# A fused attention and FFN block on one core: one root for the last normalisation, rows less means beside the power, and the last products by tile

## The chip, the cores and the metric

The kernel runs on one core of one Trainium2 chip. The metric is device time in microseconds (us) of one execution, of which several are taken; the profile is one more execution, recorded by the hardware profiler. The engines are named as in the profile: PE (TensorE, with PEld for its weight loads), DVE (VectorE), ACT (ScalarE), POOL (GpSimd) and SP (SyncE, which here only issues transfers).

## The reference

The input x holds 16 sequences of 256 rows and 256 columns, in float32. Two residual blocks follow each other, each normalised before and after:

```
x = x + layernorm(attention(layernorm(x)))
x = x + layernorm(ffn(layernorm(x)))

layernorm(x) = (x - mean(x)) / sqrt(var(x) + 1e-5)          # over the 256 columns

attention:  q = x @ Wq.T                  16 heads of 128, rotary embedding
            kp, vp = x @ Wkv.T            one key and value shared by the heads
            kh, vh = per-head factors: a cumulative sum over rows with learned decay
            k = kp * kh (rotary), v = vp * vh
            p = softmax(causal(q k / sqrt(128)));   o = p v;   o @ Wout.T

ffn:        gate, up = split(x @ ternary(w_gate_up).T)       1024 each
            h  = silu(gate) * up
            hn = h / sqrt(mean(h * h) + eps)                 # rms_norm, eps of float32
            hn @ ternary(w_proj).T
```

`ternary` quantises weights in groups of 64 to -1, 0 or 1 times the group's mean magnitude. The last layernorm works on rows that the rms_norm has scaled by one factor each, 1 / sqrt(mean(h*h) + eps).

## The kernel before

The 16 sequences go in 8 pairs. A pair and a head make a slot (128 slots, about 8.07 us each), and in each slot PE computes the scores of one head, the outputs of the head before it, the queries of the next one, and pieces of projections and of the FFN. DVE takes the exponent's maximum and the rotary products, ACT the exponents, the division by the softmax's total (L722) and the copies of outputs (L801, `oT`), POOL the products that make keys and values (L658 `kT`, L770 `vph`). SP issues nearly all transfers, among them those that transpose the probabilities.

The order on each engine is the order in which the program is written. Inside a slot there are places (`first`, `scored`, `turned`, `emptied`, `projection`, `last`), and `put(slot, place, steps, key=...)` hangs a step into one of them. The table `MOVED` shifts a step by its key, in sixths of a slot. Keys beginning with P and Q belong to the next pair's preparation (`keep` is ACT's copy of the normalised rows L391, `nor` the normalisation with POOL's power L260 and product L300), keys with T to the twelve blocks of ternary weights that are quantised during pair 0 (`narrow` L207, a POOL cast; `magnitudes` L197 on ACT; `compare` L215 to L221 on DVE; `combine` L227 to L230 on POOL; `write` L233, an ACT cast), keys with Y12 to the FFN of sequence 12.

[...]

The last normalisation never scales its rows by the rms factor: with acc the projection of the unscaled h, `inv` = (ss/1024 + eps)^-0.5 is computed on POOL (`inverse_roots`), and the rows' own factor from var(acc) * inv^2 (`last_factors`, or `end_factors` and `end_scales` for the last three). `inverse_root` (L254) is one POOL power, with an addition of eps ahead of it where one is asked for. `Rows` holds mean and variance of tiles of 128 rows: `bn_stats` (L271), `bn_aggr` (L273), `shifts` (L285: minus mean times factor, on DVE) and `apply_on_act` (L290).

The FFNs of the last three sequences, 13 (`c`), 14 (`a`) and 15 (`b`), run behind the last head in the function `end`, in an order written out by hand, with the steps of sequence 12 and of older work between them (`rest`). Each of them ends with `end_rows` (L1060): ACT scales and shifts the two tiles from PSUM, DVE adds the residual `xt` (L1076), SP stores each tile (L1077). Sequences 0 to 12 end with `finish` (L1033) and `store`.

## Time and profile before

| | |
|---|---|
| time, three executions | 1088.61, 1088.84, 1090.61 us (median 1088.84) |
| profiled execution | 1088.68 us, span of its instructions 1086.9 us |
| mean granted clock of PE | 0.996 |
| busy: PE, PEld, DVE, ACT, POOL | 1067.8, 854.5, 846.2, 736.2, 689.9 us |
| costliest PE lines (share of the chain that ended last) | L324 queries 19%, L830 output projection 18%, L670 scores 14% |
| first PE instruction, end of the last matmul, end of the span | 1.35, 1079.34, 1086.9 us |

The span runs from the first to the last recorded instruction; the execution's own time has 1.8 us more around it. The profile's chain of waits follows the work that ended last back from its end. An idle time in brackets behind a row of the timeline is the engine's idle time ahead of that row, with what released it. Ends of matmuls are modelled, so that two matmuls in a row overlap by a little.

### The profile page before, as it was taken

What the parts mean: (1) busy time and instruction counts of PE and PEld (TensorE: products, weight loads), DVE (VectorE), ACT (ScalarE), POOL (GpSimd) and SP (SyncE); (2) the same over time, 40 slices, a digit from 0 to 9 for tenths busy, and PEclk for the clock granted to TensorE, in tenths of its full rate; (3) what the DMA queues carried; (4) which work ended last, traced back from release to release, by engine and by line L of the source; (5) the groups of instructions that cost most, each with busy time, mean ns of one, the idle gap of its engine ahead of it and who ended that gap; (6) DMA issues with size and microseconds to landing.
All of it is one profiled execution on the core that took longest, in us unless ns stands there. A gap on an engine that the chain in (4) does not pass through costs nothing.

```text
span 1086.9 us, 18506 instructions
## 1 busy us (share of the span) xinstructions
PE 1067.8 (98%) x5704; PEld 854.5 (79%) x5704; DVE 846.2 (78%) x2308; ACT 736.2 (68%) x2153; POOL 689.9 (63%) x761
## 2 busy tenths in 40 slices
PE   9999999999999999999999999999999999999997
PEld 6777767788788877888778887788878888788897
DVE  6888989877887769878788777977788777877474
ACT  4877766666776658576585765866677665767664
POOL 5966897338655676458665576665865556747354
PEclk9999999999999999999999999999999999999998
DMA  6312134455444444444353444445434444443201
GB/s 230 110 53 77 61 112 155 133 159 142 141 141 133 145 136 146 139 129 151 122 154 123 151 137 131 150 132 156 131 133 144 132 133 137 145 142 97 69 1 39
DMA packets 108626, 137.35 MB, mean 126 GB/s; under 512 B 12208, under 2 KB 76208, under 8 KB 108528
## 3 DMA queue, kind: packets, MB, share of 16 engines
q1 hardware_dynamic: 105696, 129.02, 38.6%
q0 software_dynamic: 2000, 6.56, 1.8%
q8 instruction: 46, 0.75, 0.3%
q10 hardware_dynamic: 832, 0.59, 0.2%
q14 instruction: 52, 0.43, 0.1%
HBM read 88.41 MB, written 47.71 MB: 125 GB/s over the span
## 4 chain that ended last, share of the span: by engine, by line
PE 88%; DVE 6%; ACT 2%; DMA 1%; POOL 1%; issue 1%; SPq 0%; ACTq 0%; POOLq 0%; DVEq 0%
PE qps L324 19%; PE att L830 18%; PE sps L670 14%; PE ops L786 9%; PE ffn L977 6%; PE ups L884 5%; PE gps L884 5%; PE ops L793 5%; PE hg L324 1%; PE vps L324 1%; DVE turned_q L346 1%; PE kp L324 1%; DVE prob L683 1%; PE tps L756 1%; DMA moved<-sq 1%; DVE qps L354 1%
## 5 line engine op out<-in xcount | busy, mean ns | idle before, releaser
L683 DVE CUSTOM_DVE_ANT_0 prob<-sps,mask 128x128 f32<-128x128 f32 (+1 forms) x512 | 160.9, 354 | 123.2 <-PE sps L670 120.1
L801 ACT COPY oT<-ops 128x512 f32<-128x512 f32 x128 | 75.0, 586 | 258.0 <-PE ops L793 258.0
L324 PE MATMUL qps<-xnT,wq_sb 128*128 128x512 f32 x512 | 241.8, 594 | 0.8
L693 ACT ACTIVATE prob<-prob,low 128x128 f32<-128x128 f32 (+1 forms) x512 | 225.7, 444 | 18.6 <-DVE low L683 18.3
L830 PE MATMUL att<-wout_sb,oT 128*128 128x256 f32 x1024 | 237.7, 379 | 0.0
L830 PEld LDWEIGHTS att<-wout_sb,oT 128*128 128x128 f32 x1024 | 188.4, 190 | 30.2 <-issue 8.6
L770 POOL TENSOR_TENSOR vph<-vp,vh 128x512 f32<-128x512 f32 x110 | 116.2, 1056 | 128.9 <-PE ops L793 124.3
L670 PE MATMUL sps<-kT,qT 128*128 128x128 f32 (+1 forms) x1024 | 192.0, 330 | 4.3 <-DVE qT L357 2.1
L346 DVE TENSOR_TENSOR turned_q<-qps,sin_sb 64x512 f32<-64x512 f32 (+1 forms) x258 | 176.0, 682 | 15.8 <-PE qps L324 10.6
L658 POOL TENSOR_TENSOR kT<-kh,kr 128x512 f32<-128x512 f32 x128 | 165.0, 1290 | 4.2 <-PE sps L670 3.5
L722 ACT ACTIVATE even<-prob,total 128x128 f32<-128x128 f32 (+1 forms) x440 | 163.9, 447 | 1.1 <-DVE total L704 1.1
L670 PEld LDWEIGHTS sps<-kT,qT 128*128 128x128 f32 x1024 | 145.0, 191 | 21.2 <-issue 8.0
L324 PEld LDWEIGHTS qps<-xnT,wq_sb 128*128 128x128 f32 x512 | 95.2, 190 | 71.7 <-issue 61.6
L786 PE MATMUL ops<-pT,vph 128*128 128x256 f32 x440 | 131.4, 380 | 1.3 <-issue 0.7
L930 POOL TENSOR_TENSOR lo<-h,hi 128x512 fp32r<-128x512 f32 x54 | 69.0, 1277 | 89.1 <-ACT hi L928 89.1
L729 DVE STREAM_TRANSPOSE sq<-even 128x768 f32<-128x768 f32 x110 | 107.4, 977 | 13.5 <-ACT even L722 10.9
L693 ACT ACTIVATION_READ_ACCUMULATOR prob<-prob,low 128x1 f32 x512 | 97.0, 189 | 0.0
L354 DVE TENSOR_TENSOR qps<-qps,cos_sb 128x512 f32<-128x512 f32 (+1 forms) x129 | 89.4, 693 | 4.6
L793 PEld LDWEIGHTS ops<-pT,vph 128*128 128x128 f32 x440 | 83.5, 190 | 11.4
L357 DVE TENSOR_TENSOR qT<-qps,turned_q 128x512 f32<-128x512 f32 (+1 forms) x129 | 88.4, 685 | 4.5
L948 POOL TENSOR_TENSOR squares<-squares,sq 128x512 f32<-128x512 f32 x39 | 49.7, 1276 | 63.3 <-ACT sq L947 63.3
L793 PE MATMUL ops<-pT,vph 128*128 128x128 f32 x440 | 84.5, 274 | 0.0
(170 smaller groups left out, 1946.6 us busy)
## 6 DMA issues: line engine op xcount, KB each, us to landing
moved<-sq SPq DMA_DIRECT2D x110, 384.0 KB, 2.3
pT<-moved SPq DMA_DIRECT2D x440, 96.0 KB, 2.2
kh<-rows SPq DMA_DIRECT2D x126, 256.0 KB, 3.4
xt<-in_x_dram SPq DMA_DIRECT2D x15, 256.0 KB, 3.0
out_dram<-y POOLq DMA_DIRECT2D x13, 256.0 KB, 3.3
wout_sb<-in_wout_dram SPq DMA_DIRECT2D x2, 1024.0 KB, 9.7
w_gu<-in_wgu_dram POOLq DMA_DIRECT2D x8, 256.0 KB, 3.5
wq_sb<-in_wq_dram SPq DMA_DIRECT2D x1, 1536.0 KB, 10.4
```

Source lines behind the costliest of these rows:

```text
L324: nc.tensor.matmul(ps, lhs[:, c, :], rhs[:, c, :], start=(c == 0), stop=(c == EC - 1))
L346: self.engine.tensor_mul(by_sequence(self.turned[a : a + HALF, :]), by_sequence(self.src[b : b + HALF, :]), over_sequences(sin_sb[b : b + ...
L658: nc.gpsimd.tensor_mul(self.kT, self.kh, self.pair.kr)
L670: nc.tensor.matmul(sps[:, cols], self.qT[:, n0 + i * P : n0 + (i + 1) * P], self.kT[:, n0 : n0 + (i + 1) * P], start=True, stop=True,)
L683: nc.vector.tensor_tensor_reduce(out=prob[:, cols], in0=sps[:, cols], in1=mask[:, P - i * P :], scale=-SCALE, scalar=F32_MAX, op0=ALU.add, ...
L693: nc.scalar.activation(prob[:, cols], prob[:, cols], AF.Exp, bias=low[:, i : i + 1], scale=-1.0, accum_out=self.total[:, b * 2 + i : b * 2 ...
L722: nc.scalar.activation(dst, src, AF.Copy, scale=self.total[:, 2 * b + i : 2 * b + i + 1])
L770: nc.gpsimd.tensor_mul(self.vp, self.pair.vp, self.pair.vh[:, :, self.h : self.h + 1].to_broadcast([P, NT, D]),)
L786: nc.tensor.matmul(ops[:, n0 : n0 + N], self.vp[:, b * (N // P), :], early, start=True, stop=False,)
L793: nc.tensor.matmul(ops[:, n0 + P : n0 + N], self.vp[:, b * (N // P) + 1, :], late, start=False, stop=True,)
L830: nc.tensor.matmul(self.acc[:, t, :], oT[:, n0 + t * P : n0 + (t + 1) * P], wout_sb[:, h, :], start=(h == 0 and t == 0), stop=(h == H - 1) ...
L884: nc.tensor.matmul(ps[:, k, :], wgu_sb[:, c, (f0 + k) * P : (f0 + k + 1) * P], part[:, c, :], start=(i == 0), stop=(i == len(steps) - 1),)
```

## The change

Four things are changed. The first is arithmetic: (acc - mean) * inv / sqrt(var * inv^2 + e) is (acc - mean) / sqrt(var + e / inv^2), and 1 / inv^2 is ss/1024 + eps. So `sums_done` computes `floor` = e * (ss/1024 + eps) in one DVE operation, as before, and `last_factors` and `end_factors` take one power of var + floor. The power of ss, its square and two products by it are gone for every sequence.

The second is in the last three sequences: `end_rows` is cut in `end_centred`, which makes the rows less their mean (ACT for 13 and 14, DVE from PSUM for 15) and can run while POOL takes the power, and `end_rows`, where one DVE operation multiplies by the factor and adds the residual. All of these and the moments can be called for one tile of 128 rows.

The third is the order in `end`: c.ups(3) stands between the two transposes, b.pieces(3) ahead of the sums, a.pieces(1) later, and the last chunks of a and b are projected tile by tile (`project_rows`), with the moments and factors of each tile called between them.

The fourth is in the table `MOVED`.

```diff
 # in MOVED, entries changed or new
-    "P.keep1": 4, "Q.nor1": -1, "T7.wr": 4, "Y12.pj1": -1, "Y12.sq3": 3,
+    "P.keep1": 2, "Q.nor1": 5, "T7.wr": 7, "Y12.pj1": 2, "Y12.sq3": 1,
+    "T1.ma": -6, "T2.ma": -1, "T2.wr": 4,
...
+        def project_tile(self, u, k, t):
+            for i, part in enumerate(self.hi_lo[u]):
+                nc.tensor.matmul(self.acc[:, t, :], part[:, k, t * P : (t + 1) * P],
+                                 wproj_sb[:, 2 * u + k, :], ...)
+        def project_rows(self, t):
+            for k in range(2):
+                self.project_tile(FC // 2 - 1, k, t)
...
         def sums_done(self):
-            self.inv = small.tile([P, 2], F32, tag="inv", name=f"inv_{self.q}")
+            self.floor = small.tile([P, 2], F32, tag="inv", name=f"floor_{self.q}")
             nc.vector.tensor_scalar(
-                self.inv, self.ss, 1.0 / FF, RMS_EPS, ALU.mult, ALU.add
+                self.floor, self.ss, LN_EPS / FF, LN_EPS * RMS_EPS, ALU.mult, ALU.add
             )
-        def inverse_roots(self):
-            ...
         def last_factors(self):
             rows = self.last
             rows.minus_mean()
-            nc.gpsimd.tensor_mul(rows.rs, rows.mv[:, :, 1], self.inv2)
-            inverse_root(rows.rs, rows.rs, LN_EPS)
-            nc.gpsimd.tensor_mul(rows.rs, rows.rs, self.inv)
+            nc.gpsimd.tensor_add(rows.rs, rows.mv[:, :, 1], self.floor)
+            inverse_root(rows.rs, rows.rs, 0.0)
             nc.gpsimd.tensor_mul(rows.nm, rows.nm, rows.rs)
...
+        def end_moments(self, *some):
+            ...
+            for t in some:
+                nc.vector.bn_stats(part, self.acc[:, t, :])
+                nc.vector.bn_aggr(self.mv[:, t, :], part)
+        def end_factors(self, *some):
+            at = slice(some[0], some[-1] + 1)
+            nc.vector.tensor_add(self.rs[:, at], self.mv[:, at, 1], self.floor[:, at])
+            inverse_root(self.rs[:, at], self.rs[:, at], 0.0)
+            if self.q < B - 1:
+                nc.vector.tensor_scalar_mul(self.nm[:, at], self.mv[:, at, 0], -1.0)
+        def end_centred(self, *some):
+            for t in some:
+                if self.q < B - 1:
+                    nc.scalar.activation(self.y[t], self.acc[:, t, :], AF.Identity,
+                                         bias=self.nm[:, t : t + 1])
+                else:
+                    nc.vector.tensor_scalar_sub(self.y[t], self.acc[:, t, :],
+                                                self.mv[:, t, 0:1])
+        def end_rows(self, *some):
+            for t in some:
+                nc.vector.scalar_tensor_tensor(self.y[t], self.y[t], self.rs[:, t : t + 1],
+                                               xts[self.q][:, t, :], ALU.mult, ALU.add)
+                nc.sync.dma_start(out=out[self.q, t * P : (t + 1) * P, :], in_=self.y[t])
...
 def end():
         a.transpose()
+        c.ups(3)
         b.transpose()
...
         b.split()
-        c.ups(3)
         c.square(1)
...
         a.project(0)
-        a.pieces(1)
         b.project(0)
         b.pieces(1)
-        c.end_scales()
+        c.end_centred(0, 1)
         a.gates(2)
         a.gates_done(2)
+        a.pieces(1)
...
         b.add_squares(3)
+        b.pieces(3)
         a.sums_done()
-        a.inverse_roots()
         b.sums_done()
-        b.inverse_roots()
-        a.project(3)
-        b.pieces(3)
-        b.project(2)
-        a.last_moments()
-        b.project(3)
-        a.end_factors()
-        b.last_moments()
-        a.end_scales()
-        b.end_factors()
-        a.end_rows()
-        b.end_scales()
-        b.end_rows()
+        a.project_rows(0)
+        a.project_rows(1)
+        a.end_moments(0)
+        a.end_moments(1)
+        a.end_factors(0)
+        a.end_factors(1)
+        a.end_centred(0)
+        a.end_centred(1)
+        b.project(2)
+        b.project_rows(0)
+        b.end_moments(0)
+        a.end_rows(0)
+        b.end_factors(0)
+        b.project_rows(1)
+        a.end_rows(1)
+        b.end_moments(1)
+        b.end_factors(1)
+        b.end_centred(0)
+        b.end_centred(1)
+        b.end_rows(0)
+        b.end_rows(1)
```

## The prediction

> **What bounds the kernel now.** I read the page first, then the waits of PE, the chain of waits, and the timeline wherever the first two name a place. Line numbers are of the kernel before; a number with L is a line, the others are us from the span's start.

> ```profile
> PE 1067.8 (98%) x5704; PEld 854.5 (79%) x5704; DVE 846.2 (78%) x2308; ACT 736.2 (68%) x2153; POOL 689.9 (63%) x761
> PEclk9999999999999999999999999999999999999998
> ```

> PE is busy 98% of 1086.9 us and the diff takes no matmul away, so all that can be won is PE's idle time, its slow clock, and what lies behind its last matmul. PE ends at 1079.34: the tail is 7.57 us, and the idle time ahead of it sums to 11.5 us. The waits of PE say where:

> ```profile
> PE sps L670 <- DVE qT L357: 2.1, 2, 1.5
> PE sps L670 <- DVE total L704: 2.1, 3, 0.9
> PE tp_f L317 <- ACT xn_f L290: 1.4, 2, 1.3
> PE ops L786 <- ACT pT L761: 1.0, 2, 0.8
> PE tps L756 <- ACT prob L722: 0.2, 1, 0.2
> ```

> The columns are us in total, times, longest. The third row is the largest that the change touches; PE's timeline puts it at 1043, in the hand-ordered end, behind which PE has under 0.2 us of idle:

> ```profile
> 1043.21 0.33 PE L317 MATMUL tp_f<-ident,xn_f 128*128 128x128 f32 x1 [1.28 <-ACT xn_f L290]
> 1043.70 0.55 PE L317 MATMUL tp_f<-ident,xn_f 128*128 128x128 f32 x3 [0.16 <-ACT xn_f L290]
> ```

> The chain of waits gives the tail, from the last 24 projections on:

> ```profile
> 1074.86 4.49 PE ffn L977 x24
> ...
> 1079.37 0.76 DVE st_c L271 x2
> ...
> 1080.63 1.03 ACT y L1068 x2
> ...
> 1082.41 0.56 ACT y L1068
> ...
> 1083.46 0.42 DVE y L1076
> ```

> Between PE's end and the last add everything is serial on DVE and ACT, the two sequences one after the other; 3.02 us from the add's end (1083.88) to the span's end are the store.

> **Part 1: PE's gap at 1043.** The change puts c.ups(3) (8 matmuls, 0.12 us apart in L884's rows) between the two transposes. Its inputs are long there, and the 1.28 us gap holds its 0.96 us: **0.96**, since PE is filled from here to its end and the matmuls are missed nowhere later (the waits of later pieces have 0.2 to 2 us to spare in the trace). c's own last rows and a.pieces(1) change places among DVE's and ACT's work 15 to 30 us ahead of the end; SP issues the same six stores in the same order. Their readers have that slack too: nothing.

> The rest of the gap is a chain that begins ten us earlier:

> ```profile
> 1033.61 1.28 POOL L948 TENSOR_TENSOR squares<-squares,sq 128x512 f32<-128x512 f32 x1
> 1033.66 1.25 DVE L285 SCALAR_TENSOR_TENSOR nm_b<-mv_b,rs_b 128x2 f32<-128x2 f32 x1 [1.15 <-POOL rs_b L260]
> ```

> A two-column operation that takes 0.16 us at 1082.21 takes 1.25 here, and ends with POOL's add. ACT and DVE then run back to back from 1034.95 to xn_f. Y12.sq3 puts ACT's square ahead of oT_14, so this add runs before the power and POOL's fold (0.74 in its rows) stands here instead: nm_b ends 0.54 sooner, and with it xn_f: **0.54**. [...] PE's idle from 1041 to 1044 is 0.13, 1.28 and 0.16, so 1.50 of 1.57 are taken. Lower bound nothing (xn_f is late for another reason), upper 1.57.

> **Part 2: pair 0.** Four moves touch PE's small waits there.

> ```profile
> 43.70 2.00 DVE L221 SCALAR_TENSOR_TENSOR t_gu<-t_gu 128x512 bf16<-128x512 bf16 x1
> 43.85 1.28 POOL L658 TENSOR_TENSOR kT<-kh,kr 128x512 f32<-128x512 f32 x1
> 48.21 0.70 PE L786 MATMUL ops<-pT,vp 128*128 128x256 f32 x2 [0.80 <-ACT pT L761]
> ```

> L221 takes 0.69 where POOL is quiet. With Q.nor1 at 5, POOL makes a cast and kT_4 ahead of rs_a1, which may bring the blocked compare up to 0.8 us forward, and with it the scores, pT and the 0.80 us wait: 0 to 0.8. T7.wr takes a 0.62 us ACT cast from in front of the divides at 127.1 (PE waits 0.18 and 0.07 for them) into an ACT gap of 1.38 us: 0.25 to 0.45. T1.ma moves an ACT copy into a gap of 0.8 us, T2.wr costs 0.5 at one divide that PE's own 0.87 wait at 83.03 swallows, P.keep1 moves an ACT copy within slack, T2.ma leaves its engine's order as it is: nothing each; without that cover T2.wr costs its 0.5. Of 0 to 1.1 I take **0.7**.

> **Part 3: four small POOL operations per sequence gone** (power 0.70, two products, an addition of 0.2; some 1.3 us for each of q = 0 to 12). POOL is busy 63%, its first reader is `finish` a slot (8.07 us) later, and PE waits for no such tile: nothing. Y12.pj1 moves 8 matmuls behind tps_14 and leaves the 0.72 us wait at 1023.47 as it is.

> **Part 4: the tail.** Call X the end of the first 20 of the last 24 matmuls, 1078.68. Before, it goes: 4 matmuls 0.66, two bn_stats and aggregations to X+1.67, two factors and a shift to X+1.91, then for b the power (0.69) beside a's rows, ACT 1.02 to X+4.75, DVE's second add to X+5.20, and 3.02: X+8.22.

> After, tile 0 of b is complete at X, and the build shows that the four matmuls of tile 1 now wait for its bn_stats (a new PE wait): bn_stats 0.03 to 0.47, PE 0.52 to 1.18 instead of 0 to 0.66. Only those four matmuls are queued behind it. On DVE meanwhile: aggregation (0.18), a's first row, rs_b0, a's second row to X+1.50, bn_stats of tile 1 to 1.85, aggregation and rs_b1 to 2.25; two subtractions from PSUM (L1033 is the nearest row: 0.53 each, 0.43 apart) to 3.10; two final rows to X+3.91, and 3.02: X+6.93. The final operation, a product and sum over 256 columns from SBUF, has no row: between L1076's 0.43 (two inputs) and the 0.56 of ACT's pass; I take 0.45, being nearest to the add. The power of b1 (2.33 to 3.02) hides behind the subtractions with 0.1 to 0.4 us to spare; uncovered it costs 0.7 at most. Gain **1.29**, bounds 0.6 to 1.6; I count 1.25.

> **Sum.** 0.96 + 0.54 + 0.7 + 1.25 = 3.45, from the profiled execution's 1088.68 (span 1086.9 and 1.8 around it; the median of the runs is 0.16 above): **1085.2**.

> **The rivals.**

> *The slow clock falls elsewhere.* In the windows:

> ```profile
> 1075.50:1079.00 3.50, 3.50 (x19) 3.50 (x18) 1.54 (x7) 0.00 (x0) 2.51 (x5) 0.51 0.00 0
> ```

> The last columns are granted clock 0.51, DMA share, GB/s. From 1075.5 to 1078.9 PE runs at half clock, 16 projections 0.213 apart instead of 0.12: 1.4 us lost, after 2.6 us of one-column ss_late matmuls. With the end 2.2 us earlier and PE's gap filled, this stretch may miss the projections: 1083.8. [...] Against: ss_late's order is unchanged. 0.12.

> *PE's gap is not filled to profit*: silu or the split of a becomes late, PE stalls at the next user as long. Then 1.50 of the sum goes: 1086.7, no change. For: ACT and DVE run back to back in 1034 to 1042. Against: PE's next waits have slack. 0.16.

> *Slower: compares caught by POOL in pair 0.* Moving Q.nor1 and the casts shifts POOL against DVE in slots 2 to 16. Of the 24 compares (L218, L221), those at 42.42, 43.70, 113.15 and 127.30 are stretched by POOL from 0.69 to 1.4 to 2.1; some that now run free (57.9, 69.2, 84.0, 148.3) may be caught, 1.35 us each, and DVE's scores stand behind them and PE behind those. Without part 2's 0.7 the gain is 2.75: three caught give 1090.0, four 1091.3, slower by over 0.2%. For: pair 0 holds all long PE waits. Against: the changed order touches few of those slots. 0.10.

> *DVE locked out in the tail.* a's second row (two SBUF inputs) is issued while POOL takes b0's power; were it held for the power's 0.69, with PE's tile 1 behind, 0.8 of the tail's gain goes: 1086.0. Against: at 1081.22 DVE adds took 0.43 us beside that same power. [...] 0.06.

> **How the numbers follow.** My forecast has 0.56: with its unknowns (part 2 from 0 to 1.1, tail 0.6 to 1.6) 1084.4 to 1086.7. With the rivals at 1083.8, 1086.0 and most of 1086.7, the range is 1083.0 to 1087.8 with some 0.85 in it. 0.2% of 1088.84 is 2.2 us, about what a measurement of this kernel can tell from no change: faster means under 1086.66. Forecast 0.54, clock 0.12, lock 0.05 and a quarter of the gap case make 0.75; the rest of that case and the milder catches make "same" 0.17, the catches 0.08.

> **What would show it.** Right: tp_f of the last sequence with under 0.2 us of wait and ffn_13 after it about 1.5 us earlier for the whole end; nm_b under 1 us; the wait at 48.21 under 0.5; a tail of 7.0 us or less behind PE's tile-0 matmuls; PE's end near 1077. Wrong: new PE waits on L683's scores between 20 and 150, a PE gap moved to the first ups of a or b, or b1's power behind both subtractions.

## The result, and the profile after

The changed kernel takes 1085.41 us (median of 6, 1084.36 to 1087.19) against 1089.64 (median of 6, 1088.27 to 1090.61): a ratio of 0.9961, 95% interval 0.9949 to 0.9973. Forecast were 1085.2, within 1083.0 to 1087.8. The profiled execution takes 1085.46 with a span of 1083.7, 3.2 us shorter than before's 1086.9, and the forecast's 3.45 was made against that execution. The medians differ by 4.2 because three of those six runs of before lie at 1090.5; 63 later runs of it, taken beside the experiments, have medians of 1088.4 to 1088.6 and reach from 1086.98 to 1091.71. Where this scatter comes from is the subject of the last experiments.

Line numbers after the change are one higher up to L960 and differ behind it. The page's busy times of the changed kernel:

```profile
PE 1067.4 (98%) x5704; PEld 854.3 (79%) x5704; DVE 846.4 (78%) x2306; ACT 734.5 (68%) x2151; POOL 670.7 (62%) x705
```

Rows of the waits of PE (us in total, times, longest):

```profile
PE sps L671 <- DVE qT L358: 2.2, 2, 1.5
PE sps L671 <- DVE total L705: 1.6, 3, 0.9
...
PE tp_a L318 <- DVE xn_a L301: 1.1, 2, 0.8
PE ops L787 <- ACT pT L762: 0.8, 2, 0.6
...
PE ffn L981 <- DVE st_c L1064: 0.5, 1, 0.5
PE tp_f L318 <- ACT xn_f L291: 0.2, 1, 0.2
```

PE does the same work in the same busy time; POOL lost 56 operations and 19 us that nobody waits for. The 1.4 us wait for xn_f is 0.2, and a new wait of 0.5 for bn_stats has come. The wait for xn_a is longer than before's 0.3, but its longest piece, 0.76, lies at 6.94, among the loads of the start. The timeline at the two operations that led to the former gap (POOL's, DVE's) and at the gap itself (PE):

```profile
1033.04 0.73 POOL L997 TENSOR_TENSOR squares<-squares 128x256 f32<-128x256 f32 x1
...
1033.09 0.70 DVE L286 SCALAR_TENSOR_TENSOR nm_b<-mv_b,rs_b 128x2 f32<-128x2 f32 x1 [1.17 <-POOL rs_b L261]
...
1042.14 0.98 PE L318 MATMUL tp_f<-ident,xn_f 128*128 128x128 f32 x4 [0.19 <-ACT xn_f L291]
```

The two-column operation still ends with POOL's, which is now the short fold: 0.70 instead of 1.25 us. The tail in the chain of waits:

```profile
1072.78 3.61 PE ffn L981 x20
...
1076.42 0.44 DVE st_c L1064
...
1076.91 1.24 PE ffn L981 x4
...
1078.16 0.45 DVE st_c L1064
...
1079.01 0.45 DVE y L1082 x2
...
1079.71 0.14 DVE y L1089
```

The last 24 projections start at 1072.65 instead of 1074.72, and everything behind the twentieth is on DVE except PE's last four. ACT, whose passes over the rows were 1.03 and 0.56 us of the chain before, is on it no longer; POOL's power is on neither chain.

To split the span I use one mark, the start of PE's 5231st matmul (1012.39 us before, 1011.81 after), ahead of everything that the change does in `end`. Up to it 0.58 us are won (0.70 if counted from the 31st matmul, past the loads of the start); from it to the start of the last 24 projections 62.33 us became 60.84, 1.49 won; from there to the end 12.18 became 11.03, 1.15 won.

### The profile page after: what moved, and what is told of

The parts are those of the page before. It is cut to its first block, busy times and chain, and to the rows that moved or that the text cites. A ratio compares the mean times of both kernels' runs of the same rounds, so it can differ in the third digit from the quotient of the medians.

```text
span 1083.7 us, 18439 instructions
## 1 busy us (share of the span) xinstructions
PE 1067.4 (98%) x5704; PEld 854.3 (79%) x5704; DVE 846.4 (78%) x2306; ACT 734.5 (68%) x2151; POOL 670.7 (62%) x705
## 4 chain that ended last, share of the span: by engine, by line
PE 89%; DVE 8%; ACT 1%; issue 1%; POOL 0%; DMA 0%; DVEq 0%; POOLq 0%; ACTq 0%
PE qps L325 19%; PE att L831 18%; PE sps L671 14%; PE ops L787 9%; PE ffn L981 6%; PE ups L885 5%; PE gps L885 5%; PE ops L794 5%; DVE turned_q L347 2%; PE hg L325 1%; PE vps L325 1%; DVE prob L684 1%; PE kp L325 1%; DVE qps L355 1%; DVE qT L358 1%; PE tps L757 1%
```

## The experiments

The theory is the prediction's: three parts that add, PE's gap (1.5), pair 0 (0.7) and the tail (1.25). In the edits, `transpose`, `split`, `gates`, `ups`, `hidden`, `pieces`, `square` and `project` are the steps of one sequence's FFN (class `After`): its normalised rows `xn_f` are transposed into `tp_f` and split into a high and a low part, `pieces` splits h alike, `project` makes `ffn`, `fold` adds up halves of the squares on POOL (sequences 0 to 12), and `ss_late` are the sums of squares of the last three sequences, matmuls of one column. Four runs do one part alone, or the arithmetic of the middle alone; a fifth, ups3_back, takes one edit of the first part out.

**gap_alone**

```diff
 before.py
-    "Y12.sq3": 3
+    "Y12.sq3": 1
         a.transpose()
+        c.ups(3)
         b.transpose()
...
         b.split()
-        c.ups(3)
```

> The kernel before with only c.ups(3) between the transposes and Y12.sq3 at 1. Theory of three parts: the last 24 projections start 1.5 us earlier (1.3 to 1.6), the tail behind them is as before (12.2 us, less or more by what the half clock does), nm_b at 1033 under 0.8 us. Rival (the gap moves to the next late tile): under 0.5 us earlier, and a new PE wait of 0.5 us or more between 1044 and 1075.

Median 1086.95 us of 10 (nine from 1086.66 to 1087.12) against 1088.55 of 31; ratio 0.9978, 0.9967 to 0.9989. From the mark to the last 24 projections it takes 60.85 us, as the whole change does (60.84): the 1.48 us are won by these two edits. The row of tp_f in PE's waits in gap_alone:

```profile
PE tp_f L317 <- ACT xn_f L290: 0.2, 1, 0.2
```

And in its timeline:

```profile
1042.48 0.98 PE L317 MATMUL tp_f<-ident,xn_f 128*128 128x128 f32 x4 [0.20 <-ACT xn_f L290]
```

No new wait appeared behind it; the rival falls.

**ups3_back** takes the first of the two edits out of the changed kernel.

```diff
 after.py
         a.transpose()
-        c.ups(3)
         b.transpose()
...
         b.split()
+        c.ups(3)
```

> The changed kernel with c.ups(3) back behind b.split(). Theory that the filled gap also keeps the clock up: in the same clock state about 0.9 us slower than the changed kernel (1086.3 where that has 1085.4), and the idle time of PE near 1042, with the transposes about it, lets a stretch of half clock of 3.4 us fall right behind it in some executions, so that some 3 in 10 times lie 1.5 to 1.7 us above the rest. Rival (the slow stretches come at random places of the last 40 us): same share of long times as the changed kernel.

Median 1086.11 (10 runs), 0.7 above the changed kernel's, with the idle time of 1.27 us back ahead of tp_f; tp_f itself comes 0.56 us earlier than before, measured from the mark: Y12.sq3's share alone, forecast 0.54. Two of ten times (1087.61, 1087.71) lie 1.6 above the main group, fewer than the 3 in 10 expected; the changed kernel has one of six (1087.19). That does not tell the theory of the clock from its rival; spread_gap below does.

**pair0_alone**

```diff
 before.py, MOVED
-    "P.keep1": 4, "Q.nor1": -1, "T7.wr": 4,
+    "P.keep1": 2, "Q.nor1": 5, "T7.wr": 7, "T1.ma": -6, "T2.ma": -1, "T2.wr": 4,
```

> The kernel before with only the six entries of MOVED that act in pair 0 and its neighbours (P.keep1, Q.nor1, T1.ma, T2.ma, T2.wr, T7.wr). Theory of three parts: PE 0.5 to 0.7 us earlier from 200 us on, most of it from the wait at 48 and the one at 128, with 0.25 us lost and regained near 76 to 83; the rest as before. Rival (the 0.6 us seen is the start of this execution): within 0.2 us of before from 200 us on.

Median 1088.38 against 1088.55, ratio 0.9999 (0.9988 to 1.0010). Its trace shows the steps as the changed kernel's does: 0.37 us won at 48 (from the 31st matmul on), 0.52 lost near 76 and regained at 83, 0.88 won by 132. Then it gives nearly all back: 0.39 at the scores at 134, and 0.35 more by 164, where PE has a wait that before's trace has not (the first row; the other two stand in before with 0.27 and 1.45):

```profile
163.72 1.58 PE L671 MATMUL sps<-kT,qT 128*128 128x128 f32 x8 [0.27 <-DVE qT L358]
167.32 0.67 PE L787 MATMUL ops<-pT,vph 128*128 128x256 f32 x2 [0.30 <-ACT prob L694]
170.25 0.92 PE L671 MATMUL sps<-kT,qT 128*128 128x128 f32 x4 [1.38 <-DVE qT L358]
```

The first loss, 0.35 to 0.39, is in all nine profiled kernels with these entries, which stand at 0.49 to 0.62 won behind it. The second, 0.32 to 0.37, is in five of the nine and, with 0.33, in spread_pair0 below, which has not the entries; so it comes and goes by execution, and one trace can't weigh this part. All can: from the 31st matmul to the mark, the nine profiled kernels with these entries won 0.05 to 0.82 us (mean 0.55), the four others without them, beside before, 0.18 to 0.21 or lost 0.05 (mean with before 0.11). By these means the part is worth 0.44 us; they scatter so much that 0.2 either way is open.

**tail_alone** is the changed kernel with MOVED of before and c.ups(3) back: new arithmetic, new tail.

> The changed kernel with the table MOVED of before and c.ups(3) back behind b.split(): the new maths and the new tail alone. Theory of three parts that add: PE reaches the last 24 projections within 0.15 us of before's 1074.72 us, the gap of 1.28 us before tp_f is still there, the tail from that point to the span's end is 10.7 to 11.2 us instead of 12.18, so 1.0 to 1.4 us faster than before. Rival (the shorter end only pays because PE comes earlier, or the half clock falls elsewhere): under 0.5 us.

Median 1088.0 of 10 (1085.68 to 1090.68), ratio 0.9984 (0.9971 to 0.9997). The times lie in groups, and the profiled execution is one of the longest, 1090.43. Its windows tell why (the column behind the busy times is the granted clock):

```profile
1043.77:1047.18 3.41, 3.41 (x20) 3.41 (x18) 2.27 (x6) 1.48 (x3) 1.28 (x1) 0.50 0.02 5
1074.50:1081.30 6.80, 6.80 (x33) 6.80 (x33) 1.60 (x10) 0.74 (x2) 0.76 (x2) 0.50 0.00 0
```

The same windows of pair0_alone:

```profile
1044.34:1047.76 3.42, 3.42 (x19) 3.42 (x17) 2.14 (x6) 1.33 (x3) 1.28 (x1) 0.50 0.02 5
1075.06:1081.89 6.83, 6.83 (x34) 6.83 (x34) 2.14 (x9) 0.00 (x0) 2.87 (x5) 0.50 0.01 2
```

Both have a stretch of half clock behind PE's gap and two on the last projections, where before's profiled execution had one. Counted from the mark, tail_alone's stretches start 0.14 us ahead of pair0_alone's. So these two can be compared with each other: from the mark to the end tail_alone takes 76.55 us and pair0_alone, with the old tail, 77.67. The new tail is worth 1.12 us, within the 1.0 to 1.4 expected.

**maths_mid** has one power for sequences 0 to 12 and nothing else.

```diff
 before.py, for the sequences that are not late
-            self.inv = ... (ss / FF + RMS_EPS);  inverse_roots();  var * inv2, power, * inv
+            self.floor = ... (ss * LN_EPS / FF + LN_EPS * RMS_EPS);  var + floor, power
```

> The kernel before with one power instead of two for sequences 0 to 12 only; the last three keep the old maths and order. If the removed POOL operations are off the path, as the prediction has it: POOL busy about 18 us less, PE's waits the same, time within 0.2 us of before in the trace. Rival (they delay later POOL work that PE waits for): 0.5 us or more faster.

Median 1088.97 against 1088.55, ratio 1.0002 (0.9991 to 1.0014); from mark to end 74.52 against 74.51. POOL's busy time falls from 689.9 to 673.3 us, and nothing comes of it, as forecast.

Three runs take the tail apart on the changed kernel.

**rows_together**

```diff
 after.py
         b.project_rows(0)
-        b.end_moments(0)
+        b.project_rows(1)
         a.end_rows(0)
-        b.end_factors(0)
-        b.project_rows(1)
         a.end_rows(1)
-        b.end_moments(1)
-        b.end_factors(1)
+        b.end_moments(0, 1)
+        b.end_factors(0, 1)
```

> The changed kernel with b's last eight matmuls in one piece: project_rows(0) and (1) behind each other, then a's rows and b's moments for both tiles. Theory that the split's new wait of PE (0.53 us) costs what it wins: PE ends 0.5 us sooner behind the first 20 of the last 24 matmuls, DVE's moments of tile 0 come later by 0.5 to 0.9 us, and the tail is within 0.3 us of the changed kernel's 7.3 us from X. Rival, the split is worth its 0.4 us or more: tail at 7.7 us or longer.

**two_banks**

```diff
 after.py
+                if self.q == B - 1:
+                    other = ps_o.tile([P, 2, E], F32, tag="o", name="ffn_apart")
+                    self.accs[1] = other[:, 0, :]
...
-        b.project(0)
         b.pieces(1)
...
         b.gates(2)
+        b.project(0)
```

> The changed kernel with the two tiles of b's projection in two PSUM tiles (the second where c's was), so that PE's tile 1 need not wait for the moments of tile 0; b.project(0) goes behind b.gates(2) for that. If the new wait costs what the trace shows: PE's 0.53 us wait gone, PE ends 0.5 to 0.9 us sooner behind X, tail from X 6.5 to 6.9 us instead of 7.3, 0.4 to 0.9 us faster. Rival (DVE alone sets the tail, PE's end is hidden): within 0.2 us.

rows_together has a median of 1085.57 (10 runs, ratio 0.9972, 0.9962 to 0.9981), two_banks of 1085.35 (7 runs, ratio 0.9968, 0.9954 to 0.9981): with the changed kernel's 1085.41, three times the same. The profiled executions of both had the two stretches of half clock, as tail_alone has; from X to the span's end they take 6.92 and 6.95 us, and tail_alone, with split and wait, 6.95. The changed kernel's own 7.30 has another reason: its last four matmuls ran at half clock, where those of tail_alone, behind the same wait, ran at full clock. In two_banks DVE works without a pause from X on, so PE's end is hidden. The wait of 0.53 us is real, then, but removing it brings nothing where the last four matmuls run at full clock, and 0.35 us where they run at half clock, as two_banks's own did; the medians don't show it. Not splitting brings nothing either.

**ss_spread** sets the one-column matmuls of the last sums between the projections. a's last projections come before b's last sum for that.

```diff
 after.py
         a.add_squares(2)
...
         a.project(2)
...
         a.add_squares(3)
+        b.project(2)
         b.add_squares(2)
         b.square(3)
+        a.project_rows(0)
+        a.project_rows(1)
+        b.pieces(3)
         b.add_squares(3)
-        b.pieces(3)
+        a.end_moments(0)
+        a.end_moments(1)
         a.sums_done()
         b.sums_done()
-        a.project_rows(0)
-        a.project_rows(1)
-        a.end_moments(0)
-        a.end_moments(1)
...
         a.end_centred(1)
-        b.project(2)
         b.project_rows(0)
```

> The changed kernel with the 32 one-column matmuls of the last sums set between the last projections, eight at a time, instead of 24 in a row. If those 2.6 us in a row are what brings the half clock onto the last projections: no stretch of half clock before PE's end, the last projections 0.12 us apart, 1.2 to 1.6 us faster (1084.0), and less spread from run to run. Rival (the clock falls by a window that no order changes): the stretch stays, within 0.3 us.

1083.91 us, four runs within 1083.89 to 1083.94; ratio 0.9955 (0.9939 to 0.9971). The stretch of half clock in the windows of the changed kernel:

```profile
1073.75:1077.15 3.40, 2.88 (x14) 2.58 (x14) 2.07 (x11) 0.84 (x2) 1.09 (x2) 0.50 0.00 0
```

The windows of ss_spread, from ahead of the first of these sums to PE's end:

```profile
1068.00:1076.40 8.40, 7.71 (x65) 7.29 (x63) 4.64 (x18) 2.95 (x6) 1.88 (x4) 1.00 0.01 2
```

The clock stays at 1.00 to PE's end, and these four runs hardly scatter. From the mark to the end it takes 70.64 us, the changed kernel 71.87: 1.23 us. The theory holds for the last projections; the rival, a window that no order changes, falls. This is the fastest version of the study.

Four runs use ss_spread as a base. They ran on another chip than ss_spread, and scatter by up to 1.1 us there (before, beside them, by 4.5); so spans are compared from the mark on.

**spread_gap** is ss_spread with c.ups(3) back, the edit of ups3_back.

> ss_spread with c.ups(3) back behind b.split(), so that PE's gap of 1.28 us near 1042 is open again and all else is as in ss_spread, whose times do not scatter. Theory that the gap brings a stretch of half clock behind it in some executions: most times near 1084.8 (0.9 above ss_spread), a second group 1.5 to 1.7 us above that, in 2 to 4 of 10. Rival (the gap costs its idle time alone, the upper groups of before come from the last projections): all times within 0.3 us of 1084.8.

Median 1085.27 (five runs, 1084.75 to 1085.35). From the mark to the end 71.58 against 70.64: the gap costs 0.94 us, and c.ups(3) was forecast at 0.96. No second group came. For this kernel the rival holds, though not by its number: of the fifteen executions that had this gap with Y12.sq3 at 1 none is 3 us above its group, while 11 of the 63 later runs of before are.

For the gap as before has it the traces say more. In the profiles the clock changed at whole multiples of 3.413 us from the first full clock on record (last section), and the windows of this grid can be laid over PE's row. The whole gap fell into one of them in pair0_alone, and in ups3_back too; the windows, in this order (behind the length, PE's busy time):

```profile
1040.93:1044.34 3.41, 1.84 (x12) 1.18 (x12) 1.95 (x3) 2.67 (x6) 1.64 (x2) 1.00 0.00 0
1039.53:1042.94 3.41, 1.98 (x15) 1.48 (x14) 2.22 (x3) 2.67 (x6) 2.00 (x3) 1.00 0.00 0
```

PE worked 1.84 us of the first, and the next window ran at half clock (1044.34 to 1047.76, clock 0.50, under tail_alone); it worked 1.98 us of the second, and the clock stayed. Shifting the grid along the traces in steps of 0.01 us, the least work in a window here is 1.84 in the four kernels with the gap as before (for 28 to 29% of the positions), 1.98 in ups3_back and spread_gap, and 2.72 or more where c.ups(3) fills the gap. So a stretch was seen behind before's gap, in pair0_alone and in tail_alone, and none behind the shorter one; that Y12.sq3 at 1 is already enough to prevent it is the author's estimate from these windows, 1.84 against 1.98.

**spread_pair0** is ss_spread with the six entries as before.

> ss_spread with the six entries of MOVED of pair 0 as before, to weigh part 2 of the prediction where the times do not scatter. By the prediction 0.7 us slower (1084.6); by the traces of pair0_alone and the changed kernel, between 0.0 and 0.5 slower, since what is won by 133 us is partly given back at the waits near 134 and 164.

1084.71 (four runs, 1084.45 to 1084.94); from the 31st matmul to the mark it loses 0.05 us against before, where ss_spread wins 0.81. From the mark to the end the two are alike, 70.67 and 70.64. On the same chip spread_act and spread_whole, which have the entries, lie at 1084.37 and 1084.53, so by the times the part is worth 0.2 to 0.3 us, by the traces 0.44.

**spread_whole** is ss_spread with b's last eight matmuls and moments in one piece, as in rows_together, a's rows behind b's factors.

> ss_spread with b's last eight matmuls in one piece and its moments behind them. If the split by tile pays for itself at full clock: 0.3 us or more slower than ss_spread (1084.2). If its wait of PE (0.67 us in ss_spread) costs as much as it wins, as rows_together says at half clock (6.9 us behind X against 7.3): 0 to 0.4 us faster.

1084.53 (six runs, 1084.12 to 1085.26). From the mark 70.83 against 70.64: at full clock the split is worth 0.19 us, less than the 0.3 that would have spoken for it and no loss either.

**spread_act**

```diff
 ss_spread.py
         def end_factors(self, *some):
...
-            if self.q < B - 1:
+            if True:
                 nc.vector.tensor_scalar_mul(self.nm[:, at], self.mv[:, at, 0], -1.0)
         def end_centred(self, *some):
-                if self.q < B - 1:
+                if True:
                     nc.scalar.activation(self.y[t], ..., AF.Identity, bias=self.nm[...])
...
         a.end_rows(1)
+        b.end_centred(0)
         b.end_moments(1)
         b.end_factors(1)
-        b.end_centred(0)
```

> ss_spread with b's rows less means on ACT instead of DVE. In ss_spread DVE works without a pause of over 0.1 us from 1073.6 to 1079.07, so if DVE is what the tail hangs on: the two subtractions (0.87 us) go beside it and the end comes 0.3 to 0.5 us sooner (1083.5). If the power of the last tile is what ends last: within 0.1 us.

1084.37 (four runs, 1084.05 to 1084.50); 70.65 from the mark, as ss_spread. The timelines of its DVE and POOL:

```profile
1077.32 0.43 DVE L1064 BATCH_NORM_STATS2 st_c<-ffn 128x6 f32<-128x256 f32 x1 [0.21 <-ACT y L1078]
...
1078.24 0.78 POOL L261 TENSOR_TENSOR rs_c<-rs_c,minus_half 128x1 f32<-128x1 f32 x1 [0.72 <-DVE nm_c L1072]
...
1079.06 0.48 DVE L1089 SCALAR_TENSOR_TENSOR y<-y,rs_c,xt 128x256 f32<-128x256 f32 x1 [0.44 <-POOL rs_c L261]
```

DVE now waits 0.44 us for the power of the last tile, which took the place of the two subtractions. But the edit made that way longer as well: bn_stats of tile 1 starts 0.57 us behind PE's end instead of 0.28, having waited for ACT's row of tile 0, and the power takes 0.78 beside DVE's row of tile 0 instead of 0.55. From PE's end to the span's end it is 5.78 us against 5.77. So this edit is worth nothing; what the subtractions alone cost stays open.

## Why the prediction was right

- *PE's gap.* Forecast 1.50, measured 1.49 in the changed kernel and 1.48 in gap_alone; its two terms 0.94 (for 0.96) and 0.56 (for 0.54). Both profiles show the mechanism: nm_b ends within 0.02 us of POOL's operation beside it (1.25 us beside 1.28 before, 0.70 beside 0.73 after), and the chain behind it moved by as much. The forecast took all of it out of 1.57 us of idle time; 0.32 of that is still there (0.19 and 0.13), and 0.25 came out of the rows of the transposes (a's four took 0.98 before, 0.13 of it idle, and take 0.66 with no idle time).
- *Pair 0.* Taken at 0.7 from a range of 0 to 1.1, measured 0.44 as a mean over profiles. The term is mis-sized: 0.88 is won by 132 us, more than was summed, 0.52 of it by T7.wr (for 0.25 to 0.45), and what was left out is that the scores at 134 then wait and give 0.35 to 0.39 of it back. The step at 48 also went otherwise than argued. The compare L222 still runs beside kT and takes 1.98 us:

```profile
43.46 1.98 DVE L222 SCALAR_TENSOR_TENSOR t_gu<-t_gu 128x512 bf16<-128x512 bf16 x1
```

  It only starts 0.24 earlier, the compare ahead of it taking 1.10 instead of 1.36. PE's wait at 48 is 0.61, not under 0.5 as the list of signs had it, and 0.38 us are won there in all. T2.wr lost its 0.5 at 76 and PE's wait at 83 fell from 0.87 to 0.35, as reckoned.
- *POOL's operations of the middle:* nothing, and maths_mid measured nothing.
- *The tail.* Forecast 1.25 with 6.93 us behind X; 1.12 to 1.15 measured, and 6.95 where the last matmuls run at full clock. The changed kernel's 1.15 is made of 0.92 behind X and 0.23 ahead of it, and the latter is chance: 2.63 us of PE's work ahead of X ran at half clock, 3.13 before. The term that was off in the changed kernel's own execution is PE's four matmuls of tile 1, reckoned to end at X+1.18: they ended at X+1.75, since after the wait, 0.53 us as reckoned, they took 1.22 us at half clock instead of 0.66. So two signs failed in this execution: PE ends at 1078.13, not near 1077, and the tail behind X is 7.30, not 7.0 or less. The title's third item, the products by tile, is not where the gain comes from: without the split the tail is as short at half clock, and 0.19 us longer at full clock. What remains are the rows less means, which take ACT's passes off the chain, and the shorter arithmetic; this is argued from what is left over, and no run tells the two apart.
- *The rivals.* The filled gap did bring profit; pair 0 was not slower. The clock did not leave the projections: the stretch moved along with the end, 1073.75 instead of 1075.55, as did the row of 24 one-column matmuls ahead of it (from 1072.13 to 1070.05); ss_spread, which breaks them up, took 1083.91 at a clock of 1.00 to PE's end, near this rival's 1083.8. The lock in the tail did not cost its 0.8. The rows of the changed kernel on DVE and POOL at that place:

```profile
1077.44 0.47 DVE L1089 SCALAR_TENSOR_TENSOR y<-y,rs_c,xt 128x256 f32<-128x256 f32 x1
...
1077.60 0.72 POOL L261 TENSOR_TENSOR rs_c<-rs_c,minus_half 128x1 f32<-128x1 f32 x1 [1.32 <-DVE rs_c L1069]
1079.09 0.55 POOL L261 TENSOR_TENSOR rs_c<-rs_c,minus_half 128x1 f32<-128x1 f32 x1 [0.77 <-DVE rs_c L1069]
```

  DVE's operation takes its 0.47, and it is the power, second to start, that takes 0.17 longer than the 0.55 of the one at 1079.09. It ends at 1078.32, ahead of the subtractions' end, so nobody waits for it.

The difference of the medians, 4.2 against the 3.2 of the profiled executions, holds about 1 us that no part of the sum stands for: three of the six runs of before lie at 1090.5, where 22 of its 63 later runs lie above 1089.4. Of those later runs the 22 have granted clocks of 0.993 and 0.995, the other 41 of 0.996 to 0.998; that the three had more half clock in them than its usual run is the author's estimate from this, for the clocks of the six are not on record. Against the 1088.4 to 1088.6 that its later runs give, the change is worth some 3.1 us, and the parts as measured, 1.49, 0.44 and 1.13, sum to 3.06. That is 0.39 below the 3.45 that was summed, most of it pair 0's.

## What to carry to other kernels

When an engine that is nearly always busy has one gap, look for work whose inputs are ready and which has to be done anyway: eight matmuls in a hole of 1.28 us brought 0.94 of their 0.96. Follow the remainder of such a gap back along its chain; here it began ten us earlier with a two-column operation of DVE that took 1.25 us beside an addition of 1.28 on POOL. Where times of one kernel come in groups, look at the granted clock before fitting an explanation to a median: spreading 24 one-column matmuls between dense ones brought 1.2 us, as much as the whole rewritten tail, and took most of the scatter away.

## What the runs showed of the hardware

PE's time in matmuls of more than one column can be counted for each window of this grid (each matmul counted from its start to its end or the next one's start). In before, the window ahead of the stretch, 1072.13 to 1075.55, has 0.82 us of it: PE's row is busy throughout, but 2.59 us of that are one-column matmuls. In the changed kernel the window ahead, 1070.34 to 1073.75, has 1.10. In every earlier window these two profiles have 1.96 us or more, and the next window ran at full clock each time. The window at half clock itself has 3.41 in before, and full clock came behind it; in the changed kernel it has 2.89, and the next ran at half clock too. In pair0_alone 1.84 us had half clock behind it, in ups3_back 1.98 had not (the two windows under spread_gap). Across the fourteen profiles twelve windows had 1.70 to 1.84: the next ran at half clock behind two of them (the gaps of pair0_alone and tail_alone) and at full clock behind ten. So no limit can be read from these numbers; they go with the clock in the places named, and what decides it is not shown. In ss_spread, with eight one-column matmuls at a time, PE was busy for 7.71 of the 8.40 us from 1068.00 to 1076.40 at a clock of 1.00, and the four times lie within 0.05 us of each other.

By the author's estimate a stretch costs some 1.5 us (in before 16 matmuls 0.213 us apart instead of 0.12), which would make a ladder of the runs of before near 1087.0, 1088.4, 1090.0 and 1091.6. The granted clocks of its 63 later runs fall in the same groups: 0.998 in the two lowest, 1086.98 and 1087.15, 0.996 or 0.997 in the 39 from 1087.2 to 1088.9, 0.995 in the eleven from 1089.4 to 1090.3, 0.993 in the eleven above 1091.3. Profiles were seen with one stretch ahead of PE's end (before, 1088.68), with two of its windows (rows_together) and with three (pair0_alone, 1091.9); with this order of the one-column matmuls, none without, so what the lowest times had is not shown.

A two-column operation of DVE that takes 0.16 us at 1082.21 in before took 1.25 there beside a POOL addition of 1.28, and 0.70 in the changed kernel beside one of 0.73.
